# Length 1 of the LSTM stage: the product i*g moved to VectorE, and the first pair's blocks interleaved in another order

## The chip, the cores and the metric

The kernel runs on one core of a Trainium2 chip. A core has a matrix engine (TensorE, PE in the profile; its weight loads are PEld), a vector engine (VectorE, DVE), an activation engine (ScalarE, ACT) and a general engine (GpSimd, POOL). Each runs its own queue of instructions in order, and engines wait for one another through semaphores. SyncE (SP) issues the DMAs, also in order. The metric is the device time of one execution, in microseconds.

## The reference, cut to what matters

The input is 128 graphs of 64 nodes with 256 features, in fp32. Four layers follow, each added to its input and normed over the features. The first is a graph attention, the second an attention over 512 edges, the third a graph convolution with batch norms. The change lies in the fourth:

```python
h = relu(einsum('ts,bsh->bth', adj, x @ Wg0 + bg0))
h = relu(einsum('ts,bsh->bth', adj, h @ Wg1 + bg1))
for p in range(1, MAX_SKIP + 1):            # 4
    nw = Tv // p
    wins = h[:, :nw * p, :].reshape(Bv * nw, p, Hd)
    last = _lstm_last(Wih[p - 1], Whh[p - 1], bih[p - 1], bhh[p - 1], wins)
    idx = jnp.arange(nw) * p + (p - 1)
    h = h.at[:, idx, :].set(last.reshape(Bv, nw, Hd))
```

One LSTM step from a zero state, which is all there is at p = 1 ("length 1"), comes to `c = sigmoid(i) * tanh(g)` and `h = sigmoid(o) * tanh(c)`, where i, g and o are thirds of `x @ Wih.T + bias`. The forget gate has nothing to act on.

## The kernel before, in words

The tokens are kept transposed: features on the 128 partitions (two halves, k = 0 and 1), tokens along the free axis. The fourth layer works on **pairs** of groups. A group is 16 graphs, a pair 32 graphs, and there are four pairs, 0 to 3. A pair's tokens lie in two tiles' worth of columns, n = 0 and 1 (one per group), each of two halves v of 512 columns.

**Blocks.** `gcn(g, half, ...)` does the norm after the third layer and both convolutions for one block of 8 graphs; a pair needs four blocks, two for n = 0 and two for n = 1. It is a generator, and each `next` issues one step. For the first pair the steps are: scale (ACT, L1268); norm of the first half and norm of the second (PE transposes L1286, add L1292, statistics L95/L96, inverse root L86 on POOL, scaling L100 on POOL, store L1297); neighbours (PE L1254, copies L1317/L1318); two halves of the first weight product (PE L1324, bias add L1326 on DVE, relu L1328); two halves of the second (PE L1336, bias add L1339); neighbours again (PE L1254), whose relu (DVE L1347, ACT L1348) writes the pair's tile `H`. For later pairs the block is loaded from DRAM (L1272), transposed on DVE (L1236), sent out and back through DRAM (`way`, L1239 and L1241), and the two norms are steps of their own.

**Length 1.** `lstm(pair)` is a generator too. For n = 0 and then 1, and for the gates g, i, o, it issues a `Wide` gate: four results of 128x512, (m, v) for output half m and column half v. `eight` computes them with eight products (L1509). `seven` does it with seven products of sums and differences of the blocks (L1437), numbered 1 to 7, which need `column_sums(n)` of `H` (L1391 to L1394, four operations on POOL) and of the weights (`Sx`); the results are put together by copies on ACT and adds on DVE, and for product 7 one add on POOL. Products that share a bank of PSUM wait until the one before has been read: 2 follows 1, 3 follows 5, and 4 follows 7 follows 6.

The last steps of a gate (`tail`) are issued beside the products of the next gate: product 4, the activations `act`, then `after` (for i the product with g; for o the product with tanh(c), which writes `H`) and `tanh`. At the end of n = 1 the last gate has `last` instead, and length 2 begins with L1662, which reads the new `H`.

**Order.** `given` ties whatever it issues behind the last instruction of each of PE, DVE, ACT and POOL, so these four engines' orders are the program's order. DMAs are ordered by the framework's scheduler instead. The order of the first pair is written out by hand: a list of block steps before the LSTM starts, a second short list after `lstm` of pair 0 has issued its column sums, and a table (`put`) of which steps go behind which *unit* of the LSTM. In length 1 units 0, 1, 2 follow the gates g, i, o of n = 0, unit 3 ends n = 0, units 4, 5, 6 follow the gates of n = 1, unit 7 ends it, and unit 8 follows the first gate of length 2. The same table places the blocks of pair k + 1 beside pair k, the loading of weights, and the sums of the weights (`prepare`; L1192, L1203 on POOL, stores L1206).

Of the kernel before, what the change touches and what calls it, by code (L numbers as in the profile page):

```python
# [12 lines left out]
OP = mybir.AluOpType  # L13
# [28 lines left out]
def kernel(ctx: ExitStack, tc: tile.TileContext, i, out):  # L42
    nc = tc.nc
# [66 lines left out]
    def given(do, *args, **more):  # L110
        traced = nc.cur_bb.bb.instructions
        first = len(traced)
        with ExitStack() as order:
            for e in latest.values():
                order.enter_context(tc.issue_after(e))
            r = do(*args, **more)  # L116
        for t in traced[first:]:
            if t.engine in (mybir.EngineType.PE, mybir.EngineType.DVE, mybir.EngineType.Activation,
                            mybir.EngineType.Pool):
                latest[t.engine] = t  # L120
        return r
# [8 lines left out]
    with ExitStack() as two:  # L130
# [450 lines left out]
        pair = su.tile([P, EC, 4], F32, name="pair")  # L581
# [154 lines left out]
        def hidden(q, m):  # L736
            return Z[q][:, m, :] if m < 2 else Aq(q)[:, (m - 2) * QT:(m - 1) * QT]
# [15 lines left out]
        def put(q, m, p_):  # L753
            nc.scalar.activation(hidden(q, m), p_, AF.Identity, bias=b1[:, m:m + 1])
            nc.vector.bn_stats(st1[:, m, q, :], hidden(q, m))
# [299 lines left out]
        def prepare(q):  # L1055
            terms[q] = []
            later = [(k, n) for k in range(M1) for n in range(2)]

            def one():
                k, n = later.pop(0)  # L1060
                given(relu, q + 2 + n, k)
            for g in range(2):
                b = lambda k, n, g=g: hidden(q + n, 2 * g + k)
                a = lambda m, k, g=g: w2[:, 2 * g + k, m * P:(m + 1) * P]
                T = sums_in_order(b)
                next(T)
                one()
                yield
                terms[q].append((a, [SW[1][:, n, g] for n in range(4)], b, next(T)))
                one()  # L1070
                if g == 0:
                    one()
                yield
            one()
            yield
            one()
            one()
# [298 lines left out]
    def lstm(pair):  # L1376
# [9 lines left out]
        def half(n, k, v):  # L1386
            return H[:, n, k].rearrange("p t b -> p (t b)")[:, v * QT:(v + 1) * QT]
# [8 lines left out]
        class Wide:  # L1396
# [63 lines left out]
            def after(self, m, v):  # L1460

                if self.name == "i":
                    g = self.gates["g"][m][v]
                    if m and not v:
                        given(nc.gpsimd.tensor_tensor, self.t[m][v], self.t[m][v], g, OP.mult)
                    else:
                        given(nc.vector.tensor_mul, self.t[m][v], self.t[m][v], g)
                elif self.name == "o":
                    given(nc.vector.tensor_mul, half(self.n, m, v), self.t[m][v], self.gates["i"][m][v])

# [32 lines left out]

        def eight(G, rest):

            def two(m, v):
                b = lbank([QT])
                for k in range(KD):
                    nc.tensor.matmul(b, G.weight(m, k), half(G.n, k, v), start=k == 0, stop=k == KD - 1)  # L1509
                return b  # L1510

            for m in range(2):
                for v in range(2):
                    G.act(m, v, given(two, m, v))
                    next(rest, None)
            for _ in rest:
                pass

        def seven(G, rest, order):
            for j in order:  # L1520
                G.product(j)
                next(rest, None)
            for _ in rest:
                pass

        rest = iter(())
        for n in range(2):
            if n == 0:
                given(column_sums, 0)
                yield "begin", 0  # L1530
            elif pair == 0:
                given(column_sums, 1)
            gates = {}
            for name in "gio":
                G = Wide(name, n, gates)
                if name == "g" and (n == 0 or pair == 0):
                    eight(G, rest)
                    rest = iter(())
                else:
                    seven(G, rest, (1, 6, 5, 2, 7, 3) if (n, name) == (1, "o") else (1, 6, 5, 2, 3, 7))  # L1540
                    rest = G.tail()
                if (n, name) == (1, "o"):
                    G.last()
                elif name == "i" and n == 0 and pair:
                    given(column_sums, 1)
                yield "at", unit
                unit += 1
            yield "at", unit
            unit += 1

        for p in range(2, SKIP + 1):
# [197 lines left out]
            for r in range(len(runs)):  # L1749
                if p > 2:  # L1750
                    yield "gap", unit
                for s in range(p):
# [16 lines left out]
                    else:  # L1769
# [31 lines left out]
                        o = prev  # L1801
# [70 lines left out]
    parts = [gcn(n // 2, n % 2, gbank if n % 2 == 0 else lbank, "hT" if n % 2 == 0 else "xs") for n in range(4)]  # L1872
# [1 line left out]
    for p in (2, 3):  # L1874
        weights_of[0, p].room()
    given(first_sums)
    for n in [0, 0, 0, 1, 1, 0, 1, 0, 0, 1, 0, 0, 1, 1, 0, 2, 1, 3, 1, 1]:
        given(next, parts[n])
    lstms = [lstm(k) for k in range(NP)]
    next(lstms[0])  # L1880
    for n in [2, 2, 3, 3]:
        given(next, parts[n])
    next(first[0])

# [6 lines left out]
            kind, u = key if isinstance(key, tuple) else ("at", key)  # L1891
            side.setdefault((pair, kind, u), []).append(part)

    for n, u in [(2, 0), (3, 0), (2, 1), (2, 1), (3, 1), (3, 1), (2, 2), (2, 2), (3, 2), (3, 2), (2, 2), (3, 2)]:
        put(0, parts[n], u)
    put(0, first[0], 3, 4)
    put(0, first[1], 8, 13, 15)

    def gap(u):
        return "gap", u  # L1900

    def wait(u):
        return "wait", u

    for k in range(NP):
        if k:
            put(k, prepare(weights_of[k, 3]), 8)
            put(k, prepare(weights_of[k, 4]), 23)
        else:
            put(k, prepare(weights_of[k, 4]), 23, 26, 30)  # L1910
        for n in range(2):
            g = k * 2 + n
            for s in range(SKIP - 1):
                u = 34 + 4 * s + 2 * n
                put(k, final(g, s), u, u + 2)
            if k < NP - 1:
                put(k + 1, final(g, SKIP - 1), 9 + n, 12 + n)
        if k < NP - 1:
            put(k, prepare(weights_of[k + 1, 2]), 34)
            for n, keys in enumerate([  # L1920
                    [9, gap(11), 12, wait(15), 16, gap(18)],
                    [5, 9, 11, 13, 15, 19, wait(22), gap(22), gap(25), 26, gap(29)],
                    [13, 17, 19, 21, 23, 27, wait(33), gap(33), gap(36), 37, 38],
                    [21, 24, 26, 28, 30, 34, gap(40), 41, gap(44), 45, 46]]):
                block = gcn((k + 1) * 2 + n // 2, n % 2, gbank, "hT")
                if n == 0 and k:
                    put(k - 1, block, 40, 42, 43)
                    put(k, block, 0, 0)
                elif n == 0:
                    put(k, block, 3, 4, 5, 7, 8)  # L1930
                put(k, block, *keys)
    for k in range(NP):
        for kind, u in lstms[k]:
# [46 lines left out]
```

## Time and profile before

| | us |
|---|---|
| time of a run, median of 3 | 2060.67 (2058.96 to 2063.55) |
| the profiled execution | 2058.14 |
| its span, first to last instruction | 2056.4 |
| PE busy in the span | 1943.3 |
| PE busy from 760 to 861 us (pair 0: blocks and length 1) | 90.23 of 101 |
| PE busy from 861 to 911 us | 43.41 of 50 |
| PE busy from 1139 to 1184 us (length 1 of pair 1) | 42.66 of 45 |
| the same stretch of pair 2, of pair 3 | 42.66, 42.67 of 45 |

The table gives busy times of one profiled execution, by stretch of its span. A stretch that is not full of PE work holds waits of PE; the timeline of the stretch names for each instruction how long its engine had been idle before it, and which instruction released it. Since engines run their queues in order, a wait can be passed on: an engine that waits holds all that is queued behind it.

### The profile page before, as it was taken

The numbers are of one execution on the slowest core, as the hardware profiler recorded it, in microseconds if no ns is written. First come the engines' busy times: TensorE is split into PE (matmuls) and PEld (weight loads), VectorE is DVE, ScalarE is ACT, GpSimd is POOL, SyncE is SP. The second block draws the span as 40 slices with busy tenths as digits, with TensorE's granted clock in tenths as the row PEclk, the third lists the DMA queues.
The fourth block names the chain that finished last, engine by engine and source line by source line (L and its number), as shares of the span: only waits on it lengthen the run. The fifth ranks groups of instructions, "written<-read, shape, count | busy, mean of one in ns | idle before, by whom it ended". The sixth has DMA issues, their size and how long they took to land.

```text
span 2056.4 us, 31499 instructions
## 1 busy us (share of the span) xinstructions
PE 1943.3 (95%) x11449; PEld 1334.2 (65%) x11449; DVE 1243.2 (60%) x2751; ACT 987.2 (48%) x1890; POOL 893.4 (43%) x1024
## 2 busy tenths in 40 slices
PE   5999999999999989899999999999999999999997
PEld 4666667675454445477677577667577667578685
DVE  7456665564557555665566765557765557664566
ACT  2766666765345624544343544333544333544333
POOL 1123343343355543554645543435553445444264
PEclk9999999999999999999999999999999999999998
DMA  5343343322202134433242143132143032131022
GB/s 146 69 67 64 78 69 63 56 55 34 45 34 47 41 126 147 154 133 103 99 149 92 60 156 135 40 129 90 54 149 123 22 113 64 46 118 77 0 62 72
DMA packets 236539, 173.84 MB, mean 85 GB/s; under 512 B 150624, under 2 KB 213600, under 8 KB 233056
## 3 DMA queue, kind: packets, MB, share of 16 engines
q1 hardware_dynamic: 234528, 169.86, 28.9%
q8 instruction: 90, 1.47, 0.3%
q0 software_dynamic: 1024, 1.05, 0.2%
q10 hardware_dynamic: 832, 0.92, 0.1%
q14 instruction: 65, 0.53, 0.1%
HBM read 110.18 MB, written 61.60 MB: 84 GB/s over the span
## 4 chain that ended last, share of the span: by engine, by line
PE 66%; DVE 15%; POOL 7%; ACT 4%; issue 4%; DMA 2%; SPq 1%; POOLq 0%; DVEq 0%; ACTq 0%
PE l L1706 25%; PE l L1662 7%; PE pz L820 4%; PE l L1437 3%; PE pz L749 3%; PE e L346 2%; PE m L318 2%; PE g L1336 2%; PE m L321 2%; PE z L355 2%; PE pz L1017 2%; PE m L253 1%; DVE ln_st L95 1%; PE g L1324 1%; PE l L1509 1%
## 5 line engine op out<-in xcount | busy, mean ns | idle before, releaser
L1706 PE MATMUL l<-xs,wx 128*128 128x256 f32 (+1 forms) x896 | 276.9, 400 | 5.8 <-DVE gate L1725 3.9
L1706 PE MATMUL l<-hs,wh 128*128 128x256 f32 (+1 forms) x896 | 275.9, 399 | 3.7 <-DVE hs L1570 3.1
L1721 ACT ACTIVATE kept<-l 128x256 f32<-128x256 f32 (+1 forms) x224 | 88.8, 403 | 332.5 <-PE l L1706 331.1
L86 POOL TENSOR_TENSOR ln_rs<-ln_rs,mhalf 128x2 f32<-128x2 f32 (+2 forms) x98 | 86.7, 884 | 327.3 <-DVE ln_rs L98 315.8
L1706 PE MATMUL l<-H,wx 128*128 128x256 f32 (+1 forms) x672 | 210.4, 402 | 4.3 <-DVE gate L1734 3.4
L1706 PE MATMUL l<-hid,wh 128*128 128x256 f32 (+1 forms) x672 | 208.7, 399 | 0.0
L1706 PEld LDWEIGHTS l<-xs,wx 128*128 128x128 f32 x896 | 168.6, 190 | 50.8 <-issue 5.5
L1706 PEld LDWEIGHTS l<-hs,wh 128*128 128x128 f32 x896 | 169.2, 190 | 47.0 <-DVE hs L1570 5.7
L1662 PE MATMUL l<-H,wx 128*128 128x256 f32 (+5 forms) x672 | 186.1, 433 | 6.6 <-DVE H L116 4.0
L1739 ACT ACTIVATE gate<-gate,bias 128x512 f32<-128x512 f32 (+1 forms) x280 | 170.6, 657 | 42.3 <-DVE gate L1730 35.1
L1662 PEld LDWEIGHTS l<-H,wx 128*128 128x128 f32 x672 | 119.6, 191 | 67.3 <-issue 34.4
L357 ACT ACTIVATE u<-z 128x1024 f32<-128x1024 f32 x128 | 130.3, 1025 | 63.1 <-PE z L355 62.3
L1706 PEld LDWEIGHTS l<-H,wx 128*128 128x128 f32 x672 | 125.7, 190 | 42.6 <-DVE gate L1734 7.4
L1706 PEld LDWEIGHTS l<-hid,wh 128*128 128x128 f32 x672 | 127.2, 190 | 32.0 <-issue 2.4
L1729 POOL TENSOR_TENSOR gate<-gate,kept 128x256 f32<-128x256 f32 (+1 forms) x84 | 65.1, 775 | 153.3 <-DVE kept L1727 153.0
L329 DVE TENSOR_TENSOR qs<-m,qs 64x256 fp32r<-64x256 f32 x128 | 54.0, 422 | 109.3 <-ACT qs L328 107.1
L1628 ACT ACTIVATE gate<-cell 128x512 f32<-128x512 f32 (+1 forms) x88 | 58.7, 667 | 89.4 <-DVE cell L1620 63.8
L355 PE MATMUL z<-gath_r,qs 128*128 128x512 f32 x256 | 99.9, 478 | 0.6 <-ACT u L357 0.4
L1574 POOL TENSOR_TENSOR hs<-hid 128x256 f32<-128x256 f32 (+1 forms) x28 | 25.1, 896 | 172.7 <-DVE hid L1603 87.3
L1616 POOL TENSOR_TENSOR cell<-gate,cell 128x512 f32<-128x512 f32 (+1 forms) x56 | 75.5, 1369 | 28.4 <-ACT gate L1739 28.4
L1734 DVE TENSOR_TENSOR gate<-l,gate 128x256 f32<-128x256 f32 (+1 forms) x112 | 49.9, 446 | 61.4 <-POOL gate L1729 37.6
L1723 DVE TENSOR_TENSOR gate<-l,kept 128x256 f32<-128x256 f32 (+1 forms) x112 | 49.1, 438 | 56.9 <-ACT gate L1739 33.0
(376 smaller groups left out, 4092.0 us busy)
## 6 DMA issues: line engine op xcount, KB each, us to landing
wx<-sums SPq DMA_DIRECT2D x9, 2048.0 KB
wh<-sums SPq DMA_DIRECT2D x9, 1792.0 KB
way<-st SPq DMA_DIRECT2D x54, 256.0 KB
st<-way SPq DMA_DIRECT2D x216, 64.0 KB
xin<-in_x SPq DMA_DIRECT2D x16, 512.0 KB
ld<-table SPq DMA_DIRECT2D x16, 512.0 KB
x_dram<-y SPq DMA_DIRECT2D x16, 512.0 KB
x2r<-x_dram SPq DMA_DIRECT2D x32, 256.0 KB
```

What stands on the lines that cost most here:

```text
L86: nc.gpsimd.tensor_tensor(dst, dst, mhalf[:, :n], OP.pow)
L355: nc.tensor.matmul(z[:, k, :], L1[q]["qs"][c][:, s, k * P:(k + 1) * P], gath_r, start=True, stop=True)
L357: nc.scalar.activation(u, z, AF.Relu)
L749: nc.tensor.matmul(p_, w1[:, k, m * P:(m + 1) * P], Aq(q)[:, k * QT:(k + 1) * QT], start=k == 0, stop=k == KD - 1)
L820: nc.tensor.matmul(self.bank[at], lhs, rhs, start=first and n == 0, stop=n == len(self.terms) - 1, skip_group_check=True)
L1437: nc.tensor.matmul(self.bank[at], lhs, rhs, start=new, stop=True, skip_group_check=True)
L1616: nc.gpsimd.tensor_tensor(c, t, c, OP.mult)
L1662: nc.tensor.matmul(b, w.raw[0][:, k, at, m, :], x, start=k == 0, stop=k == KD - 1)
L1706: nc.tensor.matmul(self.banks[j], lhs, rhs, start=src == 0, stop=src == 1)
L1721: nc.scalar.activation(self.keep(j), b, AF.Copy)
L1729: e.tensor_tensor(t[0][:, 1], t[0][:, 1], k[5], OP.add)
L1739: given(lambda: nc.scalar.activation(dst, dst, f, bias=b))
```

## The change

1. The product i*g of the quarter (m, v) = (1, 0) moves from POOL to DVE, where the other three are. This holds for n = 0 and 1 of all four pairs.
2. In pair 0 the gate g of n = 1 is computed with `seven` instead of `eight`. Its column sums are issued before gate o of n = 0 instead of before n = 1, so the tile `H` of n = 1 must be complete by then. In pairs 1 to 3 the column sums keep their place: behind the products of gate i of n = 0.
3. The block steps of pair 0 are issued in another order. Block 2 (the third) is scaled and normed between the convolutions of blocks 0 and 1; before, blocks 2 and 3 were both normed behind them. Blocks 2 and 3 are finished at unit 1, ahead of gate o of n = 0; before, at unit 2.
4. The steps of pair 1's first block that lie in pair 0's length 1 come at units 0, 1, 3, 5, 7 instead of 3, 4, 5, 7, 8.

```diff
             def after(self, m, v):
 
                 if self.name == "i":
-                    g = self.gates["g"][m][v]
-                    if m and not v:
-                        given(nc.gpsimd.tensor_tensor, self.t[m][v], self.t[m][v], g, OP.mult)
-                    else:
-                        given(nc.vector.tensor_mul, self.t[m][v], self.t[m][v], g)
+                    given(nc.vector.tensor_mul, self.t[m][v], self.t[m][v], self.gates["g"][m][v])
...
             if n == 0:
                 given(column_sums, 0)
                 yield "begin", 0
-            elif pair == 0:
-                given(column_sums, 1)
             gates = {}
             for name in "gio":
+                if (n, name) == (0, "o"):
+                    given(column_sums, 1)
                 G = Wide(name, n, gates)
-                if name == "g" and (n == 0 or pair == 0):
+                if name == "g" and n == 0:
                     eight(G, rest)
                     rest = iter(())
                 else:
...
                 if (n, name) == (1, "o"):
                     G.last()
-                elif name == "i" and n == 0 and pair:
-                    given(column_sums, 1)
...
-    for n in [0, 0, 0, 1, 1, 0, 1, 0, 0, 1, 0, 0, 1, 1, 0, 2, 1, 3, 1, 1]:
+    for n in [0, 0, 0, 1, 1, 0, 1, 0, 0, 1, 2, 0, 0, 2, 1, 2, 1, 0, 3, 1, 1, 1]:
         given(next, parts[n])
     lstms = [lstm(k) for k in range(NP)]
     next(lstms[0])
-    for n in [2, 2, 3, 3]:
+    for n in [2, 3, 2, 3, 2]:
         given(next, parts[n])
     next(first[0])
...
-    for n, u in [(2, 0), (3, 0), (2, 1), (2, 1), (3, 1), (3, 1), (2, 2), (2, 2), (3, 2), (3, 2), (2, 2), (3, 2)]:
-        put(0, parts[n], u)
+    for u, order in enumerate([(3, 2, 2, 3, 3), (3, 3, 2, 3)]):
+        for n in order:
+            put(0, parts[n], u)
...
                 elif n == 0:
-                    put(k, block, 3, 4, 5, 7, 8)
+                    put(k, block, 0, 1, 3, 5, 7)
                 put(k, block, *keys)
```

The order of the instructions on each engine after the change, as the built program has it, is used in the prediction: it follows from these lists.

## The prediction

> **What bounds the kernel now.** I read the page's busy times first, then who waits for whom on PE after 860 us (where the first pair's length 1 is about to end), then the timeline around each wait found there. Pairs are numbered 0 to 3, lines are those of the kernel before.
>
> The page:
> ```profile
> PE 1943.3 (95%) x11449; PEld 1334.2 (65%) x11449; DVE 1243.2 (60%) x2751; ACT 987.2 (48%) x1890; POOL 893.4 (43%) x1024
> ```
> PE is the bound: only 113 us of the 2056.4 us span are free, so a change pays by taking PE work away or by ending a PE wait. One 128x512 product is two passes; the first passes of successive products follow 0.86 us apart (L1437 at 818.51, 819.37 us), which is its price.
>
> PE's waits from 860 us on (total, times, longest):
> ```profile
> PE g L1254 <- POOL A L100: 6.3, 3, 4.6
> PE l L1662 <- DVE H L116: 4.0, 4, 1.0
> PE l L1437 <- ACT wh L116: 4.0, 3, 1.3
> ```
> These three are what the change touches. The second occurs at the end of every pair's length 1, the third once in pairs 1 to 3, the first in pair 0 alone.
>
> Timeline of pair 1, the third wait (start, duration, engine, line, [idle before <- releaser]):
> ```profile
> 1155.30 1.75 DVE L116 TENSOR_TENSOR cell<-cell,hid 128x512 f32<-128x512 f32 x1
> ...
> 1157.69 0.72 ACT L116 ACTIVATE wh<-wh,bias 128x512 f32<-128x512 f32 x1 [1.22 <-DVE wh L116]
> 1158.17 0.68 DVE L116 TENSOR_TENSOR wh<-wh,hs 128x512 f32<-128x512 f32 x1
> 1158.27 1.73 POOL L1394 TENSOR_TENSOR wx<-H,wx 128x512 f32<-128x512 f32 x1
> ...
> 1159.95 1.26 POOL L116 TENSOR_TENSOR wh<-wh,hs 128x512 f32<-128x512 f32 x1
> 1161.24 0.63 ACT L116 ACTIVATE wh<-wh 128x512 f32<-128x512 f32 x1 [1.27 <-POOL wh L116]
> 1161.78 0.58 ACT L116 ACTIVATE wh<-l 128x512 f32<-128x512 f32 x1
> 1162.41 1.12 PE L1437 MATMUL l<-H,wih 128*128 128x512 f32 x2 [1.33 <-ACT wh L116]
> ```
> POOL's i*g at 1159.95 holds ACT's tanh, the tanh holds the copy behind it, and the copy holds PE. The same product at the end of length 1:
> ```profile
> 1179.07 1.72 POOL L116 TENSOR_TENSOR wh<-wh,hs 128x512 f32<-128x512 f32 x1
> ...
> 1180.82 0.63 ACT L116 ACTIVATE wh<-wh 128x512 f32<-128x512 f32 x1 [2.13 <-POOL wh L116]
> 1181.36 1.93 ACT L116 ACTIVATE gate<-gate,bias 128x512 f32<-128x512 f32 x3
> 1182.71 0.69 DVE L116 TENSOR_TENSOR H<-gate,wh 128x512 f32<-128x512 f32 x1 [2.44 <-ACT gate L116]
> ...
> 1183.45 3.29 PE L1662 MATMUL l<-H,wx 128*128 128x256 f32 x14 [1.01 <-DVE H L116]
> ```
> The longest wait, POOL's timeline in pair 0, and what PE's clock made of it (columns: stretch, its length, busy us and instructions of PE, PEld, DVE, ACT, POOL, granted clock, DMA):
> ```profile
> 866.68 0.73 POOL L1570 TENSOR_TENSOR xs<-H 128x256 f32<-128x256 f32 x1
> ...
> 869.38 1.06 POOL L1575 TENSOR_TENSOR xs<-H,xs 128x256 f32<-128x256 f32 x1
> 870.40 0.69 POOL L86 TENSOR_TENSOR ln_rs<-ln_rs,mhalf 128x2 f32<-128x2 f32 x1
> ```
> ```profile
> 869.00:873.00 4.00, 1.20 (x33) 1.06 (x33) 0.85 (x1) 1.00 (x2) 3.10 (x5) 0.50 0.14 47
> ```
> The second norm of pair 1's first block (L86, L100) stands behind the four input sums; PE waits 4.58 us for it until 871.80, then runs at clock 0.50 and needs 4.62 us from L1662 (872.97) to the first L1706 (877.59); pair 1 needs 3.55 for the same (1187.77 to 1191.32).
>
> **What the Trainium skill says.** "SBUF — State Buffer", section "SBUF: two separate sides": VectorE with two SBUF inputs and GpSimd share a port pair as an exclusive lock; who starts first keeps it for the instruction, the other blocks. The trace agrees: two DVE products of 0.68 between POOL's sums last 3.17 together, POOL's 1.27 become 1.72, and they take turns; adds with a PSUM operand keep 0.68. "TensorE: Matmul & The Clock Gate", section "Why this matters for your kernels", asks for no PE gap over about 3 us; here the gap of 4.58 halves the clock, one of 1.27 before 834.89 does not.
>
> **The change, part by part.**
>
> *i*g on DVE, pairs 1 to 3, n = 0.* POOL loses 1.26 us, DVE gets 0.68. In pair 1 the product needs ACT's 1157.69 + 0.72 = 1158.41, and now stands ahead of the other product. POOL's L1394 has no DVE product in its way and starts at about 1158.27, so DVE blocks until 1159.5. Two products end at 1160.8, the add of o's seventh product behind them at 1161.4 instead of 1159.45, which holds PE's product 4 of o (1160.06) to 1161.45. Two tanh follow to 1162.0, the copy to 1162.5: PE at 1162.55 instead of 1162.41, +0.15. Bounds: -1.0 if DVE gets the lock first, +0.5. I take +0.15, since 0.14 us separate the two starts.
>
> *n = 1, all pairs.* DVE's product runs at 1177.30, POOL's gate add then takes the lock as before to 1179.1, the other product follows to 1179.7, three short DVE operations to 1181.5, ACT's gate to 1182.25, the H product to 1183.0: PE's wait of 1.01 becomes 0.6, -0.4. Bounds -1.0 (PE is then bound by its own 18 passes ending at 1182.45) and +0.3. Pairs 1 to 3 together: 3 x (0.15 - 0.4) = -0.8.
>
> *Pair 0.* I walked PE's new order with the old durations, from 782.2 us, where the orders part. Work from there to the first L1662: before 67.0 us, after 66.1, since the eight products of g (n = 1) become seven (-0.86).
> - Block 2's transposes now lie inside block 1's convolution. The norm (0.68 + 0.7 + 0.3 + 0.3, about 2.0 on DVE) sits ahead of each bias add, so the second relu comes at 789.1 where PE is ready at 787.8: +1.3. Half a microsecond more at block 2's first add. Gone: 0.23 + 0.88 + 0.86 before block 3's neighbours, with the half-block pauses some 3.4 (blocks 2 and 3 are normed while g's products run), and 1.27 for H at 833.6. The o gate of n = 0 then starts at about 825.1 with H of n = 1 complete at 826.3.
> - POOL: n = 1's column sums 826.4 to 832.5, in turn with DVE's two products. DVE's add for o's seventh product ends at 834.65, so o's fourth waits 0.95; the transpose of the next block's second half (ACT 1.05) is ahead of the copy: 1.3 more, and 0.3 behind. g of n = 1 ends at 839.7.
> - DVE is now behind. In i, POOL's L1203 (4 x 1.27 from 835.9) takes turns with the H products, and g's fourth product needs the add behind them: 844.2 where PE is ready at 842.25, +1.95. i ends at 847.65. The first norm of pair 1's block, now on DVE between i and o, has two operations caught by L1203 for wh (845.5 to 851): +1.5, then 0.7 for o's last. L1662 starts at 857.4, 1.1 later than the 856.28 of before; the saved product and waits are spent here.
> - The end: +1.2 behind the DVE queue, as before. L1662 resumes at 862.5 (before 861.34) and ends at 865.8.
> - Now the large part. That first norm is long done, and the second (DVE 863.7 to 865.7, POOL 0.7 + 1.1) stands before the input sums: L1254 ends at 868.1, not 873.04. No gap over 3 us is left, so L1662 x16 takes 3.5: the first L1706 at 871.6 instead of 877.59, **-6.0**. The input sums (3.8 after 867.7) are ready at 871.5, in time.
>
> *Queues.* On SP the p = 2 weight load goes behind block 2's stores (791 instead of 780.72); its sums start at 835.9, so 1 MB landing some 4 us later is hidden. The second transpose's way out now stands behind the first sums' store, which waits for L1203 until 842.2. In before that store's traffic ran from 833.9 to 839, so the way lands at about 850; the second sums' store goes at 851 and took some 5 (846.5 to 851.5); the way back lands at about 858.5. DVE wants it at 863.7: 5 us of cover. If the cover is gone, each microsecond of lateness costs one, on DVE and POOL alike, for both stand still behind it. The column sums of n = 1 in pairs 1 to 3 keep their place.
>
> Sum: -6.0 - 0.8 = -6.8. The profiled execution took 2058.14 us (span 2056.4 and 1.7 around it), so it would take 2051.3; it stood 2.5 below the median of 2060.67, which becomes **2053.9**. All after pair 0's length 1 shifts with PE, whose other waits there are short (the one of 3.9 us, g L1861 <- DVE hd, is at the kernel's end and shifts too).
>
> **Rivals.**
> - *The lock costs little.* If DVE and POOL hardly meet, L1662 starts near 851, the second norm is bound by the transfer at 858.5 + 4.5 = 863.0 for L1254, 10 us earlier; the first L1706 at 866.6. With -1.0 in each other pair: about -12.5, 2048. For it: PE's bare work would end at 850. Against it: the 3.17 and 1.72 above.
> - *Swallowed.* DVE, 0.57 busy in 760 to 861, gets two products and four adds more in pair 0 and PE follows it: another 3 to 5 us of waits in n = 1, so -2, about 2058.5. For it: I find five new waits; against it: the second norm's place alone is worth the 4.58 gap and 1.1 of clock.
> - *Slower: the transfer.* The second norm is now ahead of the input sums on POOL and of the cell products on DVE. L1706 starts 9.1 us after the way back lands (norm 2.0, POOL 1.8, L1254's end, 3.5, throttled 1.1). Break-even is a landing at 868.5, with the other pairs 869.3, against my 858.5. It would need L1203 for wh to finish 11 us late; at 15 late the kernel takes 2065. Against it: POOL was busy 30.9 of the 56 us from 825 to 881.
>
> **How the numbers follow.** Forecast 0.62, lock costs little 0.15, swallowed 0.15, transfer 0.08. The likeliest gives 2053.9; its own bounds (-3.5 to -10) are 2050.5 to 2057. To leave 2 in 10 out I reach into both neighbours: 2047.5 to 2059. 0.2% (4.1 us) is about what a measurement can tell from no change. Faster by over it: 0.15 and most of the forecast, 0.77; within: 0.15; slower: 0.08.
>
> **What would show it.** Right: no wait over 2 us of L1254 for POOL near 865, clock near 1.0 there; 22 products instead of 23 from g of n = 1 on; new waits of L1437 for DVE's adds between 833 and 855; at pairs 1 to 3 the wait of L1437 for ACT of 1.3 replaced by one for DVE's gate add of about 1.4, and L1662's wait about 0.6. Wrong: DVE waiting for the transfer ahead of the second norm, or L1662 in pair 0 starting before 853 or after 860.

## The result, and the profile after

| | us |
|---|---|
| changed kernel, median of 5 runs | 2051.47 (2049.59 to 2051.53) |
| kernel before, beside it, 5 runs | 2060.67 (2058.96 to 2063.55) |
| ratio, with its 95% interval | 0.9952 [0.9937, 0.9966] |
| profiled execution before, after | 2058.14, 2051.53 |
| span before, after | 2056.4, 2049.7 |

The change makes the kernel 9.2 us faster by the medians, and 7.0 to 13.0 by the interval of the ratio; the forecast was 6.8, to 2053.9, with a range of 2047.5 to 2059. So the time lies well inside the range, and the gain was put a little too low.

Who waits for whom on PE in the changed kernel, from 855 us on (total, times, longest; L1656 and L1700 are L1662 and L1706 of before):

```profile
PE l L1437 <- DVE gate L116: 3.4, 3, 1.1
PE l L1656 <- DVE H L116: 2.7, 4, 0.9
...
PE g L1254 <- POOL A L100: 1.0, 2, 0.5
```

Compared with the three lines that the prediction shows of before, the 6.3 us of L1254 have become 1.0. The wait of L1437 has changed its releaser (ACT's copy then, DVE's add for product 7 now) and little of its size. The timeline where pair 0 goes into length 2 shows how the first came about:

```profile
862.55 3.29 PE L1656 MATMUL l<-H,wx 128*128 128x256 f32 x14 [0.91 <-DVE H L116]
...
863.62 0.68 DVE L1292 TENSOR_TENSOR x2r<-st,x2r 128x512 f32<-128x512 f32 x1
...
866.39 1.52 POOL L100 TENSOR_SCALAR A<-x2r,ln_rs 128x256 f32<-128x256 f32 x2
...
867.88 0.73 POOL L1564 TENSOR_TENSOR xs<-H 128x256 f32<-128x256 f32 x1
867.97 0.46 PE L1254 MATMUL g<-bdT,A 64*64 64x64 f32 x16 [0.50 <-POOL A L100]
...
868.36 3.72 PE L1656 MATMUL l<-H,wx 128*128 128x256 f32 x16
...
871.91 0.59 PE L1700 MATMUL l<-H,wx 128*128 128x256 f32 x2
```

L1292, the first operation of the second norm, shows no wait for its transfer; POOL scales (L100) ahead of the first input sum (L1564); PE waits twice for half a microsecond, and from L1656 x16 to the first L1700 it is 3.55 us (868.36 to 871.91) where it was 4.62.

**Where the time went.** The start of the first L1336 differs between the two traces (778.65 and 780.06) though nothing ahead of it is changed. So I count from there: the offset of an event is its start less that of the first L1336 in the same trace.

| offset, us | before | after |
|---|---|---|
| first L1662 / L1656 of pair 0 | 77.63 | 77.54 |
| first L1706 / L1700 of pair 0 | 98.94 | 91.85 |
| last store of the output | 1270.51 | 1262.48 |

Almost nothing is won up to length 2 (0.1), then 7.0 in the fourteen microseconds to the first L1700, and 0.9 after that. In pairs 1 to 3 the stretch from length 1's first products (L1509, L1505) to the place where L1662 resumes takes 44.28, 44.28 and 44.27 us before and 43.86, 43.86 and 43.85 after: 0.42 each, 1.3 in all. The rest of the length is equal within half a microsecond.

The 0.1 is two things that cancel. The busy times of the two kernels from the same point (3.35 us after L1336 starts) to the start of length 2, and over 861 to 911 us (columns as in the prediction):

```profile
782.00:856.28 74.28, 69.82 (x563) 38.14 (x561) 42.90 (x74) 37.72 (x61) 33.90 (x33) 1.00 0.42 146
861.00:911.00 50.00, 43.41 (x232) 34.41 (x233) 30.55 (x62) 18.86 (x37) 26.82 (x31) 0.93 0.32 112
```
```profile
783.41:857.60 74.19, 68.87 (x561) 36.86 (x560) 48.29 (x85) 35.97 (x58) 37.35 (x36) 1.00 0.43 152
861.00:911.00 50.00, 48.05 (x252) 36.61 (x252) 34.03 (x61) 21.66 (x40) 29.90 (x32) 1.00 0.30 109
```

Ahead of length 2, PE has 0.95 us less to do and idles 0.86 more (5.32 against 4.46), while DVE is 5.4 us busier. Behind it PE's clock is 1.00 instead of 0.93.

### The profile page after: what moved, and what is told of

The parts are those of the page before. It is cut to its first block, busy times and chain, and to the rows that moved or that the text cites. A ratio compares the mean times of both kernels' runs of the same rounds, so it can differ in the third digit from the quotient of the medians.

```text
span 2049.7 us, 31505 instructions
## 1 busy us (share of the span) xinstructions
PE 1943.6 (95%) x11447; PEld 1332.9 (65%) x11447; DVE 1256.3 (61%) x2763; ACT 987.6 (48%) x1892; POOL 883.8 (43%) x1017
## 3 DMA queue, kind: packets, MB, share of 16 engines
q0 software_dynamic: 1024, 1.05, 0.2%
## 4 chain that ended last, share of the span: by engine, by line
PE 68%; DVE 17%; ACT 5%; POOL 4%; issue 4%; DMA 1%; SPq 0%; DVEq 0%; POOLq 0%; ACTq 0%
PE l L1700 25%; PE l L1656 7%; PE l L1437 4%; PE pz L820 4%; PE e L346 3%; PE m L318 2%; PE pz L749 2%; PE g L1336 2%; PE m L253 2%; PE m L321 2%; PE z L355 2%; PE pz L1017 2%; PE g L1324 2%; DVE ln_st L95 1%; DVE cell L1614 1%
## 5 line engine op out<-in xcount | busy, mean ns | idle before, releaser
L1700 PE MATMUL l<-xs,wx 128*128 128x256 f32 (+1 forms) x896 | 277.0, 400 | 5.7 <-DVE gate L1719 4.2
L1700 PE MATMUL l<-hs,wh 128*128 128x256 f32 (+1 forms) x896 | 276.5, 399 | 2.9 <-DVE hs L1564 2.1
L86 POOL TENSOR_TENSOR ln_rs<-ln_rs,mhalf 128x2 f32<-128x2 f32 (+2 forms) x98 | 86.4, 882 | 338.1 <-DVE ln_rs L98 334.9
L1700 PE MATMUL l<-H,wx 128*128 128x256 f32 (+1 forms) x672 | 210.5, 402 | 4.3 <-DVE gate L1728 3.4
L1700 PE MATMUL l<-hid,wh 128*128 128x256 f32 (+1 forms) x672 | 208.8, 399 | 0.0
L1700 PEld LDWEIGHTS l<-xs,wx 128*128 128x128 f32 x896 | 168.6, 190 | 50.7 <-issue 5.8
L1700 PEld LDWEIGHTS l<-hs,wh 128*128 128x128 f32 x896 | 169.2, 190 | 46.8 <-DVE hs L1564 4.7
L1656 PE MATMUL l<-H,wx 128*128 128x256 f32 (+5 forms) x672 | 185.2, 431 | 4.9 <-DVE H L116 2.7
L1656 PEld LDWEIGHTS l<-H,wx 128*128 128x128 f32 x672 | 118.8, 190 | 65.5 <-issue 34.2
L1700 PEld LDWEIGHTS l<-H,wx 128*128 128x128 f32 x672 | 125.7, 190 | 42.6 <-DVE gate L1728 7.4
L1700 PEld LDWEIGHTS l<-hid,wh 128*128 128x128 f32 x672 | 127.2, 190 | 32.0 <-issue 2.6
```

The lines of the kernel that those rows point to most:

```text
L86: nc.gpsimd.tensor_tensor(dst, dst, mhalf[:, :n], OP.pow)
L1656: nc.tensor.matmul(b, w.raw[0][:, k, at, m, :], x, start=k == 0, stop=k == KD - 1)
L1700: nc.tensor.matmul(self.banks[j], lhs, rhs, start=src == 0, stop=src == 1)
```

## The experiments

The table has all runs. "Idle" is PE's idle time from 3.35 us after L1336 to the start of length 2; the ratio is to the kernel before on the same chip. Line numbers shift by a few lines from kernel to kernel; operation and tiles tell which line of before is meant.

| run | idle | offset of length 2 | of the first L1706 / L1700 | of the last store | ratio, 95% interval |
|---|---|---|---|---|---|
| before | 4.46 | 77.63 | 98.94 | 1270.51 | |
| e9, before again | 4.42 | 77.59 | 98.80 | 1270.82 | 1.0000 [0.9992, 1.0009] |
| after | 5.32 | 77.54 | 91.85 | 1262.48 | 0.9952 [0.9937, 0.9966] |
| e8, after again | 5.30 | 77.52 | 91.83 | 1261.85 | 0.9947 [0.9933, 0.9960] |
| e1, product alone | 4.45 | 79.26 * | 100.77 * | 1271.43 * | 0.9996 [0.9988, 1.0004] |
| e2, steps alone | 4.88 | 79.12 * | 93.54 * | 1264.94 * | 0.9962 [0.9948, 0.9976] |
| e3, steps undone | 4.23 | 76.13 | 99.75 | 1269.96 | 0.9979 [0.9972, 0.9985] |
| e4, weight sums earlier | 3.02 | 74.66 | 88.69 | 1258.74 | 0.9934 [0.9920, 0.9947] |
| e5, eight products kept | 3.08 | 76.77 * | 90.78 * | 1261.52 * | 0.9936 [0.9922, 0.9949] |
| e6, product on POOL | 5.06 | 77.02 | 91.45 | 1263.87 | 0.9949 [0.9935, 0.9962] |
| e7, fourth sum later | 2.99 | 74.65 | 88.66 | 1257.73 | 0.9931 [0.9917, 0.9944] |
| e10, sums earlier, eight | 1.21 | 73.22 | 87.23 | 1257.75 | 0.9938 [0.9924, 0.9952] |
| e11, recurrent sums tripled | 14.51 | 87.64 | 101.75 | 1272.21 | 1.0000 [0.9991, 1.0008] |
| e12, best | 1.19 | 73.20 | 87.22 | 1256.72 | 0.9928 [0.9915, 0.9942] |

\* In these three traces PE's granted clock was 0.50 for one piece of 3.41 us ahead of length 2 (from 808.63 us in e1, 806.32 in e2, 846.08 in e5) and 1.00 in the rest of that stretch, a mean of 0.98. In the others it was 1.00 throughout (0.95 in e11, behind a long wait). Half of 3.41 us is 1.7; against before the stretch is 1.6 us longer in e1 and 1.5 in e2. So about 1.5 to 1.7 us of each starred offset is this clock. In e1, the 3.41 us ahead of the fall, the piece at half clock, and the whole stretch:

```profile
805.22:808.63 3.41, 1.53 (x56) 1.08 (x56) 0.69 (x1) 0.60 (x1) 3.04 (x6) 1.00 0.76 241
808.63:812.04 3.41, 3.41 (x20) 1.74 (x21) 0.69 (x1) 1.19 (x2) 0.00 (x0) 0.50 0.66 208
784.63:860.54 75.91, 71.46 (x563) 38.90 (x561) 42.55 (x75) 37.46 (x60) 32.64 (x32) 0.98 0.42 147
```

In the whole stretch PE executes as many instructions as in before (x563) and idles as long, but is busy 71.46 us instead of 69.82.

**The two kernels once more (e8, e9).** No edit.

> The changed kernel once more, beside the others on one chip. If the gain is that of the trace (8.0 us from the first L1336 to the end, 6.7 in the span), the ratio to before is 0.9955 to 0.9968; 0.9952 was measured first. In its trace the first L1700 should start 91 to 93 us after the first L1336; a spread of over 1.5 us between two traces of one kernel would mean that single steps of under 1.5 us can't be read from the difference of two traces.

> The kernel before once more. If its first trace stands for its usual run, the first L1706 starts 98.9 us after the first L1336, PE waits 4.6 us for POOL's second norm and the last store starts 1270.5 after L1336. If the first trace was a lucky one (its run of 2058.1 is 2.5 below the median), one of these is 1 to 3 us later here; the ratio is 1 within 0.0015 either way.

The ratio came out at 0.9947, a little below what was expected from the trace, with an interval that reaches into that range. Up to the first L1700 the offsets repeat within 0.15 us, at the last store within 0.65. Where the clock falls in one trace and not in the other, they do not, as the stars say. The first trace of before was not a lucky one from L1336 on.

**The product alone (e1).** The kernel before, with the first hunk of the diff only.

> The kernel before with one part of the change: the product i*g of quarter (1, 0) on DVE, in all pairs. Theory A (the lock between DVE and POOL decides): PE's wait at n = 1's start in pairs 1 to 3 only changes its name (1.33 us for ACT becomes about 1.1 for DVE's gate add, PE resumes within 0.2 us of before), the wait at the end of length 1 falls from 1.0 to 0.6 in each pair; together -1 to -2 us. Rival B (the product on POOL was what PE waited for): both waits go, 3 x 2.3 + 1.0 = -8 us.

PE's waits from 861 us on:

```profile
PE g L1254 <- POOL A L100: 6.1, 2, 4.9
...
PE l L1437 <- DVE gate L116: 3.3, 3, 1.1
...
PE l L1658 <- DVE H L116: 2.4, 4, 0.6
```

The waits in pairs 1 to 3 are those of the changed kernel, as theory A had it, and the long one in pair 0 is untouched. By the ratio it is worth 0.8 us, with an interval from 2.5 faster to 0.8 slower, which neither shows nor excludes the 1 to 2 expected. That the lock costs little and the product alone brings a large gain is out.

**The steps alone (e2).** The kernel before, with the last hunk only:

```diff
-                    put(k, block, 3, 4, 5, 7, 8)
+                    put(k, block, 0, 1, 3, 5, 7)
```

> The kernel before with one part of the change: the five steps of pair 1's first block at units 0, 1, 3, 5, 7 instead of 3, 4, 5, 7, 8. Theory A (the gain is the second norm's place ahead of the input sums on POOL): L1254's wait of 4.58 us falls to 1 us or less, the clock stays at 1.0, -4.5 to -6 us, and nothing else of note. Rival B (the gain comes from the blocks' interleaving and the saved product): -1 to +1 us, since the norm then waits for its transfer or DVE instead.

The ratio stands for 7.8 us (interval 5.0 to 10.7), more than was expected. The wait of L1254 is 1.0 in two, as in the changed kernel. With the clock's 1.5 to 1.7 us taken off, length 2 begins at about 77.5, as in before and after, and L1706 at about 91.9, as in after. By the traces one line of the diff makes the gain of pair 0.

**The steps undone (e3).** The changed kernel with that line turned back.

> The changed kernel with those five steps back at units 3, 4, 5, 7, 8. Theory A: the wait of L1254 of some 4 to 5 us and the low clock behind it come back, +5 to +6 us against the changed kernel, so -3 to -4.5 us against before. Rival B: within 1.5 us of the changed kernel, about -8 us against before.

It is 5.6 us slower than the changed kernel by the two ratios, as the first theory said. The timeline of what PE waits for:

```profile
862.17 1.74 SPq L1241 DMA_DIRECT2D st<-way  x4
...
867.27 0.73 POOL L1565 TENSOR_TENSOR xs<-H,xs 128x256 f32<-128x256 f32 x1
868.09 0.73 POOL L1569 TENSOR_TENSOR xs<-H,xs 128x256 f32<-128x256 f32 x1
868.55 0.81 DVE L1292 TENSOR_TENSOR x2r<-st,x2r 128x512 f32<-128x512 f32 x1 [4.53 <-DMA st<-way]
...
870.65 1.14 POOL L86 TENSOR_TENSOR ln_rs<-ln_rs,mhalf 128x2 f32<-128x2 f32 x1 [1.83 <-DVE ln_rs L98]
...
872.50 1.25 PE L1254 MATMUL g<-bdT,A 64*64 64x64 f32 x32 [6.05 <-POOL A L100]
```

Length 2 starts 1.5 us earlier than in before, and L1706 0.8 later. The input sums were done before POOL's L86 could begin; what holds the second norm here is its transfer, issued on SP at 862.17 and used at 868.55. In the kernel before the same transfer, issued at 860.67, held L1292 for 1.05 us only, and the sums did the rest (L98 ended at 868.11, L86 started at 870.40). So the old place of the steps had two bounds, one behind the other, and the change removes both: in the changed kernel the way back is issued at 852.78, 10.8 us before its use.

The trace gives e3 a gain of 0.7 us at the last store (against the mean of the two traces of before), the runs one of 4.3, interval 3.1 to 5.8. Part of the difference may lie in which executions were traced: the two of before (2058.14 and 2059.42) lie 2.5 and 1.9 us below the medians of their kernel's runs, that of e3 (2058.87) only 0.2. The rest stays open, so what the other parts of the change are worth together is not settled: next to nothing by the traces in pair 0, 3.1 to 5.8 us in all by the runs.

**Weight sums earlier (e4).** The changed kernel, and

```diff
-    put(0, first[0], 3, 4)
+    put(0, first[0], 0, 1)
```

> The changed kernel with the sums of the p = 2 weights (L1203 on POOL, eight operations) at units 0 and 1 instead of 3 and 4, where POOL was idle for 17 us and DVE's operations read PSUM. Theory A (DVE's SBUF products take turns with L1203 in n = 1 and PE waits behind them): the wait of 1.77 us for DVE's hs add and most of the 0.9, 0.8 and 0.4 go, the first L1656 comes about 3 us earlier, -2.5 to -3.5 us against the changed kernel, so about -12 against before. Rival C (PE waits for the added operations of DVE themselves, not for the lock): no change against the changed kernel, within 1 us.

PE's waits ahead of length 2 in the changed kernel, then in e4:

```profile
PE l L1437 <- DVE hs L116: 1.8, 1, 1.8
PE l L1437 <- DVE gate L116: 1.3, 2, 0.8
PE l L1437 <- ACT wh L116: 0.9, 1, 0.9
PE l L1437 <- DVE wx L116: 0.4, 1, 0.4
```
```profile
PE l L1437 <- DVE gate L116: 1.2, 1, 1.2
PE l L1437 <- ACT wh L116: 0.9, 1, 0.9
```

With POOL's eight L1203 out of the way of n = 1, the waits for DVE's hs and wx adds are gone, and length 2 starts 2.9 us earlier. The waits for the gate add and for ACT's copy, which were to go for the most part, stay at 1.2 and 0.9. The hs and wx adds have an operand in PSUM and keep their 0.68 us; they stood on DVE behind products and norm operations that got longer beside POOL: two H products took 3.28 us beside L1203 (838.76) and take 1.27 in e4 (841.44). The ratios put e4 2.7 to 3.7 us ahead of the changed kernel, but their intervals overlap; the last store is 3.4 ahead.

**Eight products again (e5, e10).** The changed kernel (e5) and e4 (e10) with

```diff
-                if name == "g" and n == 0:
+                if name == "g" and (n == 0 or pair == 0):
```

> The changed kernel, with g of n = 1 in pair 0 back at eight products and no fourth add behind a wait. Theory (this stretch is set by DVE and POOL, not by the product saved): PE's work grows by 0.86 us, but DVE has four adds of 0.68 fewer and the wait of 1.8 for DVE's hs add goes; 0.5 to 1.5 us faster than the changed kernel, ratio to before about 0.9947. Rival (each product counts in full): 0.9 us slower than the changed kernel, ratio about 0.9957, and the first L1656 0.9 us later after the first L1336.

> The version with earlier weight sums, and g of n = 1 in pair 0 back at eight products. With POOL's weight sums out of this stretch, the wait for DVE's hs add is gone there already. Theory (the product saved counts once nothing else sets the stretch): 0.5 to 1 us slower than the earlier weight sums alone, the first L1656 0.9 later after the first L1336 (75.5). Rival (the four adds saved still count more): 0.5 to 1 us faster, L1656 at 74 or less.

In e5 length 2 starts 0.75 us earlier although 3.41 us ran at half clock; PE idles 3.08 instead of 5.32. The wait for DVE's hs add is gone, but one of 2.2 for ACT's copy, in place of 0.9, is left, and the clock falls right behind it. In e10 I expected a loss of 0.9 and got a gain of 1.4 up to length 2: the rival was right. At the last store 1.0 is left of it, and the ratios (0.9938, and 0.9934 in e4) can't tell. The waits of e10 in the same stretch:

```profile
PE l L1656 <- DVE H L116: 0.6, 1, 0.6
...
PE l L1437 <- ACT wh L116: 0.3, 1, 0.3
```

The wait for DVE's gate add is gone and that for ACT's copy is down from 0.9 to 0.3 (the 0.6 lies behind the start of length 2). Product 4 of the gate before is issued among the products of the next gate. With `seven` it comes behind three of them, and has to wait for its gate's add of product 7; with `eight` it comes behind six, 5.3 us of PE work, and the add is done. The 0.86 us of PE work that the eighth costs by its price are less than the 1.8 of idle time it saves (3.02 to 1.21). So, by the traces, the part of the change that saves work on PE loses time.

**The product back on POOL (e6).** The changed kernel without the first hunk.

> The changed kernel, with the one i*g product back on POOL in every pair. Theory (the product counts 0.4 us in each pair, at the end of n = 1): 1 to 2 us slower than the changed kernel, ratio to before 0.996 to 0.9965, with L1656's wait for DVE's H back at about 1.0 and L1437's wait for ACT of 1.3 in place of that for DVE's gate add. Rival (with the norms moved, POOL is what the second half waits for and the product is worth most of the gain): 5 to 7 us slower than the changed kernel, ratio 0.998 to 0.999.

The ratios of e6 and e8, on one chip, are 0.4 us apart, which their intervals can't tell from 1 to 2; the 5 to 7 of the rival are out. The trace shows the step sharply: 44.27 us for each of pairs 1 to 3, as in before, and in pair 0 length 2 begins 0.5 us earlier than with the product on DVE. The product on DVE costs half a microsecond in pair 0 and brings 0.42 in each of the others. At the last store e6 is 1.7 us behind the changed kernel's two traces, of which these explain 0.8.

**The fourth column sum later (e7).** e4, and for n = 1 of every pair L1394 leaves `column_sums` and is issued on its own, behind o's sixth product and the tail that runs beside it:

```diff
-            e.tensor_tensor(T[:, 3], half(n, 1, 0), T[:, 1], OP.subtract)
+            if n == 0:
+                fourth(n)
...
                     G.last()
+                elif (n, name) == (0, "o"):
+                    given(fourth, 1)
```

> The version with earlier weight sums, and besides the fourth of POOL's column sums of n = 1 (L1394) put behind o's gate add. Theory (it is the port lock with L1394 that makes two DVE products last 2.25 us and so holds PE 1.1 us in each of pairs 1 to 3): the two products take 1.4 us, PE's wait for DVE's gate add falls from 1.1 to 0.6 or less, about 1.5 us faster than with the earlier weight sums alone, unless the H products now meet L1394. Rival (the wait is for PE's own seventh product, not for the lock): the two products get shorter but PE's wait stays at 1.1, and the time is the same within 0.5.

Pair 1 in the changed kernel, then in e7:

```profile
1152.45 1.27 POOL L1394 TENSOR_TENSOR wx<-H,wx 128x512 f32<-128x512 f32 x1
...
1152.63 2.24 DVE L116 TENSOR_TENSOR wh<-wh,hs 128x512 f32<-128x512 f32 x2 [0.19 <-ACT wh L116]
1154.80 0.68 DVE L116 TENSOR_TENSOR gate<-l,wh 128x512 f32<-128x512 f32 x1
...
1155.53 1.12 PE L1437 MATMUL l<-wx,wih 128*128 128x512 f32 x2 [1.12 <-DVE gate L116]
```
```profile
1146.23 1.29 DVE L116 TENSOR_TENSOR wh<-wh,hs 128x512 f32<-128x512 f32 x2 [0.19 <-ACT wh L116]
1147.44 0.68 DVE L116 TENSOR_TENSOR gate<-l,wh 128x512 f32<-128x512 f32 x1
...
1148.18 1.12 PE L1442 MATMUL l<-wx,wih 128*128 128x512 f32 x2 [0.17 <-DVE gate L116]
...
1149.50 1.27 POOL L1399 TENSOR_TENSOR wx<-H,wx 128x512 f32<-128x512 f32 x1
...
1149.83 2.09 DVE L116 TENSOR_TENSOR H<-gate,cell 128x512 f32<-128x512 f32 x2
```

Without L1394 at their side the two i*g products take 1.29 us instead of 2.24, and PE's wait falls by 0.95: it is this meeting that makes the wait. Part of it comes back, since L1394 (L1399 here) now meets the two H products, which take 2.09, and L1442 then waits 0.5 for a later add. Net, the stretch of each pair takes 43.6 instead of 43.87: 0.8 in all, where 1.5 was expected. The ratios (0.9931, and 0.9934 in e4) don't tell the two apart.

**The transfer made late (e11).** The changed kernel, with the four L1203 of the recurrent half in pair 0 done three times over:

```diff
-            for dst, a, b, op in ((S3, a11, a21, sub), (S1, a21, a22, add), (S2, S1, a11, sub), (S4, a12, S2, sub)):
+            ops = ((S3, a11, a21, sub), (S1, a21, a22, add), (S2, S1, a11, sub), (S4, a12, S2, sub))
+            for dst, a, b, op in ops * (3 if (self.p, n) == (2, 1) else 1):
```

> The changed kernel, with the four weight sums of the recurrent half in units 3 and 4 of pair 0 done three times over, so that POOL is busy about 10 us longer, their store goes that much later, and the way back, which stands behind it on SP, is issued at about 861.5 instead of 851.3. Theory (the cover is some 5 to 6 us, and behind it each microsecond counts): the second norm's first operation starts at about 866 instead of 862.1, L1254 waits over 3 us for it, and with the clock lost behind that gap the kernel is 4 to 7 us slower than the changed one, ratio 0.997 to 0.9985. Rival (the path behind it has more slack than that): within 1.5 us of the changed kernel.

It cost all of the gain (ratio 1.0000), twice what was expected, and by another way:

```profile
850.35 13.85 POOL L1204 TENSOR_TENSOR wh<-wh 128x512 f32<-128x512 f32 x10
...
864.15 1.26 POOL L116 TENSOR_TENSOR wh<-wh 128x512 f32<-128x512 f32 x1
...
864.63 3.99 SPq L1242 DMA_DIRECT2D st<-way  x4
...
865.45 0.69 DVE L116 TENSOR_TENSOR wh<-l,wh 128x512 f32<-128x512 f32 x1 [7.49 <-POOL wh L116]
...
866.79 2.07 PE L1438 MATMUL l<-wx,wih 128*128 128x512 f32 x2 [9.62 <-DVE wx L116]
...
874.11 0.69 DVE L1293 TENSOR_TENSOR x2r<-st,x2r 128x512 f32<-128x512 f32 x1
```

POOL's own add for product 7 of gate i stands in POOL's queue behind the sums; DVE waits 7.49 us for it, and PE 9.62 for an add queued on DVE behind that. All of length 2 moves with PE, so the transfer, issued at 864.63, was in time again when L1293 came at 874.11. The run says nothing of what a late transfer costs, except that it isn't late alone; it says that POOL has almost no slack in this stretch.

**The best version (e12).** e7 with the eight products of e5.

> Earlier weight sums, the fourth column sum behind o's gate add, and g of n = 1 in pair 0 back at eight products. Theory (with eight products the waits of L1437 for DVE's gate add and ACT's copy in pair 0, 2.1 us with the weight sums alone, fall to 0.3 for 0.86 of work, whatever happens in the other pairs): 1.0 to 1.4 us faster than with the fourth sum later alone, the last store 1256.5 us after the first L1336, ratio 0.9925 to 0.993. Rival (the fourth sum, put later, had removed the same wait in pair 0 already, so that the eighth product counts in full): the first L1656 at 75.5 after L1336 and 0.9 slower, ratio about 0.9935.

The theory came out, and the rival (length 2 at 75.5) is out. Length 2 starts at 73.20, where e10 has 73.22: in pair 0 the later sum does nothing, with seven products (74.65 in e7, 74.66 in e4) or with eight, and the eight bring their 1.4 in full up to there. The waits left there are the 0.6 and 0.3 of e10. The last store is at 1256.72, 1.0 ahead of e7 and 5.4 ahead of the mean of the two traces of the changed kernel. The ratio of 0.9928 isn't told apart from e7's 0.9931 by the intervals; against the kernel before it is 14.9 us, against the changed kernel some 4 to 5.

## Why the prediction was right, and where its sums were off

- **Norm ahead of the input sums, clock kept.** The bulk, and right in size: from the start of length 2 to the first L1700 the walk (the prediction's step through PE's new order) had 14.2 us (857.4 to 871.6), the trace has 14.31; before took 21.31. e2 and e3 tie it to the one line that moves the steps. The Trainium skill's "TensorE: Matmul & The Clock Gate", section "Why this matters for your kernels" (no PE gap over about 3 us), agrees as far as long gaps go: with gaps of 4.6, 4.8, 4.9, 6.1 and 9.6 us (before, e9, e1, e3, e11) the clock of 861 to 911 us is 0.93, 0.93, 0.93, 0.90 and 0.90, without them 1.00. It is not enough: ahead of length 2 the clock fell to 0.50 for 3.41 us in e1 and e2 behind gaps of 0.9 us at most, and in e5 behind one of 2.2. There the measurement decides.
- **The reason given for the long wait** was half of it. I took the four input sums to be what the second norm stood behind. e3 shows the transfer of the way back as the next bound. In before L86 could have started at 868.11 at the earliest, behind the transfer, and started at 870.40: by this estimate, moving the norm ahead of the sums on POOL alone would have won about 2.3 of the 4.58 us. The size came out because the edit moves the transfer too, and the paragraph on the queues had followed it.
- **Pair 0 up to length 2: +1.1 predicted, -0.1 measured.** This is the term of the sum that was off, 1.2 of the difference. The walk named eight new waits: 1.3 and 0.5 in the convolutions, 0.95, 1.3 and 0.3 at o, 1.95 at g's fourth product, 1.5 and 0.7 at the norm between i and o: 8.5 in all. The trace has seven, of 0.3, 0.4, 0.5, 0.9, 1.8, 0.8 and 0.4: 5.1. They are in the right places and in the right order, and nearly each was put too large; those behind the norm in the convolutions most (0.7 for 1.8), since I put a whole norm ahead of each add. (The paragraph on "swallowed" speaks of five; the walk has eight.) As the net is off by 1.2 only, what the walk took off for the old waits must have been too much as well, by some 2.2; which of them isn't shown. The saved product is spent on them, as was said; e5 and e10 add that it would have been better not saved.
- **The lock in pairs 1 to 3: -0.8 predicted, -1.3 measured.** L1662's wait fell from 1.01 to 0.60, as predicted. The other place was put at +0.15 and is -0.02: the two DVE products took 2.24, not 2.4, and PE waited 1.12, not 1.4. The bounds held this. The Trainium skill's "SBUF — State Buffer", section "SBUF: two separate sides" (VectorE with two SBUF operands and GpSimd exclude each other for whole instructions), is borne out by e7: the same two products last 2.24 beside L1394 and 1.29 without it.
- **Which queues are moved past.** The stores and the transfer were in time, as the forecast had it. The way back had been put at 858.5 and need at 863.7; use was at 863.62, without a wait. The trace's DMA packets settle the landing: the last of the 512 packets of 512 bytes that are the way back ends at 859.12, 4.5 us ahead of the use, where 5 were forecast. In before and e3, where DVE waited for it, the last ends at 864.53 and 867.91, 0.9 and 0.6 us ahead of the use. The break-even of the slower rival wasn't tested: e11 missed it.
- **The sum.** 1.2 and 0.5 more than forecast make 8.5 instead of 6.8. The traces give 8.5 as well (1270.67 less 1262.17, the means of two traces each at the last store), and the intervals of both ratios contain it, while the forecast's 6.8 lies outside them. No error was made up for by luck: both terms that were off were off to the same side. The rival "the lock costs little" gave 2048, not far below 2051.47, but its mechanism (length 2 starting near 851, the norm bound by the transfer) did not occur. Of the waits of "swallowed" another 3 to 5 us would have been needed; there were fewer than forecast, not more.

## What to carry to other kernels

When a PE wait sits behind a long chain (transfer, norm, scaling), ask which of the engines' queues it stands in and move the whole chain ahead by units of the program, not one operation: here both the queue of POOL and the transfer were late, and one line of the order was worth 7 of the 8.5 us in the traces. Ask of a product saved on PE whether PE sets the pace there: in pair 0, where VectorE and GpSimd did, it came back as idle time, twice over. Compare two traces from an event that both reach by the same instructions, and check the granted clock piece by piece first: offsets at equal clock repeated within 0.15 us up to the first L1700, while one piece of 3.41 us at half clock moved them by 1.5 to 1.7.

## What was not expected of the hardware

- A clock of 0.98 over 75 us was in truth one piece of 3.41 us at 0.50, behind short waits. e1 and e2 share the order of the blocks with before, and its waits there (0.88 and 0.86 us at 803.51 and 805.37 in before), but before kept 1.00 in both its traces. In each trace the clock's changes from the one shortly before the first L1336 to 2020 us lie whole multiples of 3.41 us apart, and these pieces lie elsewhere in the program from trace to trace. PE was busy for 0.04 to 0.49 of the piece ahead of each of the eight falls in that stretch (0.45, 0.49 and 0.40 in e1, e2 and e5). Of the other pieces at full clock, only three were under half, 0.43 in e3 and 0.48 in after and in e11, and the clock stayed. So the falls went with PE's idle time summed over such a piece, and not with one gap alone; where exactly the line lies isn't shown.
- The 25 runs of before beside e10 spread over 7.5 us, and the spread goes with the mean granted clock: the four at 0.986 took 2058.77 to 2059.27 us, the eight at 0.983 2062.9 to 2064.47.
- The first L1336 started between 777.11 and 782.05 us in the traces although all kernels issue the same work ahead of it. That is more than most single edits here are worth.
- In e11 more work on POOL, eight operations of 1.27 or 10.2 us, put length 2 off by 10.1 us (77.54 to 87.64), although no product of length 1 reads its result: the order of a queue alone passed on some 9 of the 10.2. About 0.9 of the 10.1 is clock (L1438 took 2.07 us behind the wait of 9.62, where two passes took 1.12).
